# The setup of a fused decoder layer moves its loads into the places of the attention values, and batch 0 may load its values after the first half of them is made

## The chip, the cores and the metric

The kernel runs on one core of one Trainium2 chip. The metric is the device time of one execution in microseconds (us), lower is better. Unless said otherwise, times within a run are counted from the start of the profiled span.

The engines are called as the profile calls them: PE is TensorE (matrix products and transposes; PEld is its weight load), DVE is VectorE, ACT is ScalarE, POOL is GpSimd, and SP is the queue from which this kernel issues all its DMAs, in order.

## What is computed

The reference is a decoder layer in float32 on x of 16 batches x 512 tokens x 256 channels:

```
x = layernorm(x + self_attention(x))
x = layernorm(x + cross_attention(x, ctx))     # ctx: 16 batches x 64 rows x 256
x = layernorm(x + mixture_of_experts(x))       # 8 experts, 1024 hidden units each
```

The self attention is linear: per head, the products of keys and values over the tokens, for two sets of weights, are multiplied elementwise, and the queries are multiplied by that state. The cross attention, which the change touches, has 16 heads of 64 channels:

```
q = x @ Wq.T;  k, v = split(ctx @ Wkv.T)
attn = softmax(q k^T / 8 + mask)               # over the 64 context rows, per head
out = (attn v, heads side by side) @ Wout.T + b_out
```

In the expert layer each of the 8 experts takes the first 1024 tokens with a positive routing weight, in the order of the tokens.

## The kernel before, in words

**The work.** The batches go through the layer one by one, in stages that overlap. A setup makes what all batches need from the context. `context_keys` makes the keys and writes them to a DRAM scratch (`k_dram`). `output_weights` transposes Wout. `context_values` makes the values already multiplied by Wout, head by head, which the kernel calls v Wout, and writes them to `vo_dram`, in two halves: `context_values(0)` for batches 0 to 7 and `context_values(1)` for batches 8 to 15. So the cross attention of a batch ends in one large product of its probabilities with v Wout (L845, `ps_x`), and no output projection follows.

**A half of the values.** It has eight rounds (r = 0 to 7, two heads each). A round makes the values of 128 channels for 512 context rows (`context_rows`, L445, `ps_kv`), copies them to a tile `st`, and one round later `times_wout` multiplies them by Wout: for four groups g of two batches and two heads h it does one product each (L496, `ps_vo`). The eight results are copied by `evac` from PSUM to tiles `vst`, by ACT and DVE in turn (L186, L188), and SP writes them to `vo_dram` (L505). A `vst` holds two groups g, so a round uses two of these tiles and has four writes, of 64 partitions each.

**The places.** Tiles come from pools, and a tag in a pool has a fixed number of places; a new tile takes the place that is free first, and whoever writes it first waits for the last reader of the old tile. The tag "vo" of the pool `wk2` has six places of 4224 bytes per partition. `vst` uses them in the setup, and so do the batches' values `vo` later: `load_vo` (L789) reads a quarter of the heads and half of the context rows of one batch as one tile, in four DMAs of 32 partitions. A batch has eight such tiles: six are loaded ahead, the other two after the first two are used. The setup's other loads, the context `cn` (L424), the weights `nat` (L434) and `nato` (L528), use the tag "cn" of the pool `setup`, which has two places. That pool is closed when the routing of batch 0 begins, and the experts' pool takes its memory.

**The order of the work.** The program is written by a planner. Each stage is a generator (a stream); the class `Model` estimates what each traced instruction takes on its engine, and `weave` always continues the stream that is due first by its plan and is not waiting for something. The order that results is fixed for PE, DVE, ACT and POOL (`in_order`). The DMAs on SP are ordered by the framework's scheduler. A DMA on SP also waits for the DMA eight issues before it, since eight completion semaphores are used in turn. The eight PSUM banks (`bank`) are shared by all stages.

**What the change's steps touch.** `cross_attention` (L773 and following) first starts `load_vo` six times for every batch but batch 0; then it makes the scores (L819, `ps_sim`), the softmax in four steps per batch (L825 to L827, L805 to L809, ending in `pT`), and the product L845. Batch 0 waits after its softmax until `("values", 1)` is set, that is, until the second half has been traced, and loads its values only then. `all_routing` closes the setup's pool after batch 0's cross attention. `ranks` at the end counts the tokens of each expert with two products by constant matrices, `ones` and `before` (L898, L900), which POOL makes at the start of the program. The experts' first weights, `wi` and `wo_`, are loaded at L979 and L984 and first used at L941 (`ps_h`).

Of the kernel before, what the change touches and what calls it, by code (L numbers as in the profile page):

```python
# [9 lines left out]
FP = mybir.dt.float32  # L10
# [3 lines left out]
ALU = mybir.AluOpType  # L14
# [4 lines left out]
P = 128  # L19
# [97 lines left out]
def decoder_layer(  # L117
# [25 lines left out]
    nc = tc.nc  # L143

    B, S, C = x.shape
    J = context.shape[1]
    NT = S // P
    NC = C // P
# [11 lines left out]
    GB = 2  # L160
# [21 lines left out]
    def evac(dst, src):  # L182

        flip[0] ^= 1
        if flip[0]:
            nc.scalar.copy(dst, src)  # L186
        else:
            nc.vector.tensor_copy(dst, src)  # L188
# [7 lines left out]
    def col(name, src):  # L196
# [11 lines left out]
    eps = const.tile([P, 1], FP, tag="eps", name="eps")  # L208
    nc.gpsimd.memset(eps, EPS)

    ones = const.tile([P, P], FP, tag="ones", name="ones")
    nc.gpsimd.memset(ones, 1.0)

    before = const.tile([P, P], FP, tag="before", name="before")
    nc.gpsimd.affine_select(
        out=before, in_=ones, pattern=[[1, P]], compare_op=ALU.is_gt, fill=0.0,
        base=0, channel_multiplier=-1,
    )


    not_last = const.tile([P, 1], FP, tag="not_last", name="not_last")
    nc.vector.tensor_scalar(not_last, ident[:, P - 1:P], -1.0, 1.0, ALU.mult, ALU.add)
# [58 lines left out]
    with ExitStack() as att:  # L281
# [138 lines left out]
        BJ = B * J  # L420

        def load_context(sp, q):
            t = sp.tile([P, 4, C], FP, tag="cn", name="cn")
            nc.sync.dma_start(  # L424
                out=t,
                in_=context.rearrange("b j c -> (b j) c")[q * 512:(q + 1) * 512, :].rearrange(
                    "(i p) c -> p i c", p=P
                ),
            )
            return t  # L430

        def load_wkv(sp, r4):
            t = sp.tile([P, 4, C], FP, tag="cn", name="nat")
            nc.sync.dma_start(out=t, in_=x_wkv[r4 * 512:(r4 + 1) * 512, :].rearrange("(r p) c -> p r c", p=P))  # L434
            return t

# [49 lines left out]
        def context_values(q):  # L486


            def times_wout(r, st):
                for g in range(NG):  # L490
                    if g % 2 == 0:
                        vst = wk2.tile([P, 2, 2, CX], FP, tag="vo", name="vst", bufs=6)
                    for h in range(2):
                        hd = slice(h * J, (h + 1) * J)
                        ps = bank(f"ps_vo{h}")
                        nc.tensor.matmul(  # L496
                            ps[:, :CX], st[hd, g * P:(g + 1) * P], held["xwoutT"][hd, r, :], start=True, stop=True
                        )
                        evac(vst[:, g % 2, h, :], ps[:, :CX])
                    if g % 2 == 0:  # L500
                        continue
                    g0 = q * NG + g - 1
                    out_ = vo_dram[g0 * GB:(g0 + 2) * GB].rearrange("(g b) j h c -> b j g h c", b=GB)
                    for bl in range(GB):
                        nc.sync.dma_start(  # L505
                            out=out_[bl, :, :, r * 2:(r + 1) * 2, :].rearrange("j g h c -> j g (h c)"),
                            in_=vst[bl * J:(bl + 1) * J].rearrange("p g h c -> p g (h c)"),
                        )

            last = None  # L510
            for r in range(NP):
                st = context_rows(NP + r, q)
                yield
                if last is not None:
                    times_wout(*last)
                    yield
                last = r, st
            yield WAIT
            times_wout(*last)
            yield  # L520
            held["values", q] = True

        def output_weights():

            xwoutT = held["xwoutT"] = sp.tile([P, NP, CX], FP, tag="xwoutT", name="xwoutT", bufs=1)
            for hf in range(2):
                nato = sp.tile([P, NC, INNER // 2], FP, tag="cn", name="nato")
                nc.sync.dma_start(  # L528
                    out=nato,
                    in_=x_wout[:, hf * 512:(hf + 1) * 512].rearrange("(r p) c -> p r c", p=P),  # L530
                )
                for i2 in range(2):
                    ps = bank("ps_wo")
                    for i in range(2):
                        for oc in range(NC):
                            nc.tensor.transpose(
                                ps[:, i * C + oc * P:i * C + (oc + 1) * P],
                                nato[:, oc, (i2 * 2 + i) * P:(i2 * 2 + i + 1) * P], ident,
                            )
                    r = hf * 4 + i2 * 2  # L540
                    evac(xwoutT[:, r:r + 2, :C], ps.rearrange("p (i c) -> p i c", i=2))
                ps = bank("ps_wo")
                for i in range(NP // 2):
                    for oc in range(NC):
                        nc.tensor.matmul(
                            ps[:, i * E:(i + 1) * E], nato[:, oc, i * P:(i + 1) * P], m[:, oc, C:],
                            start=(oc == 0), stop=(oc == NC - 1),
                        )
                r = hf * NP // 2
                nc.vector.tensor_copy(  # L550
                    xwoutT[:, r:r + NP // 2, C:], ps[:, :NP // 2 * E].rearrange("p (r e) -> p r e", e=E)
                )
                yield
# [219 lines left out]
        def cross_attention(b, x1, x1T):  # L773
# [17 lines left out]
                    )  # L791
                vos.append(t)

            if b:
                for _ in range(6):
                    load_vo()

# [29 lines left out]
                beside(cross_st, softmax(t, s))  # L829
            yield from until(lambda: len(ready) == NT)  # L830
            yield from until(lambda: made(probsT))
            if b == 0:

                while ("values", 1) not in held:
                    yield 2.0
                for _ in range(6):
                    load_vo()
            yield from until(lambda: made(*vos))
            ps = [bank("ps_x") for _ in range(NT)]
            for c in range(8):  # L840
                for i in range(NH // 4):
# [44 lines left out]
        def ranks():  # L886

            place = wk1.tile([P, 6, NTT, E], FP, tag="kq", name="ranks")  # L890
            pos, tot, cum, nxt, start, rank = (place[:, i] for i in range(6))


            nc.vector.tensor_single_scalar(pos, w_all, FLT_MIN, ALU.is_ge)
            posf = pos.rearrange("p t e -> p (t e)")
            yield
            ps_tot = bank("ps_tot")
            nc.tensor.matmul(ps_tot, ones, posf, start=True, stop=True)  # L898
            ps_in = bank("ps_in")
            nc.tensor.matmul(ps_in, before, posf, start=True, stop=True)  # L900
            nc.vector.tensor_copy(tot.rearrange("p t e -> p (t e)"), ps_tot)
            nc.vector.tensor_copy(rank.rearrange("p t e -> p (t e)"), ps_in)
            yield
            src, s = tot, 1
            while s < NTT:
                nc.vector.tensor_copy(nxt[:, :s, :], src[:, :s, :])
                nc.vector.tensor_add(nxt[:, s:, :], src[:, s:, :], src[:, :NTT - s, :])
                src, nxt, s = nxt, (cum if src is tot else src), s * 2
                yield
            nc.vector.tensor_sub(start, src, tot)  # L910
            nc.vector.tensor_add(rank, rank, start)
            nc.vector.scalar_tensor_tensor(w_sel, rank, float(CAP), w_all, ALU.is_lt, ALU.mult)
            NB = B - HEAD_B
            least = small.tile([P, NB], FP, tag="least", name="least")
            nc.vector.tensor_reduce(
                least, start.rearrange("p (b t) e -> p b t e", t=NT)[:, HEAD_B:, 0, :], AX.X, ALU.min
            )
            nc.vector.tensor_single_scalar(least, least, float(CAP), ALU.is_lt)
            n_f = small.tile([P, 1], FP, tag="n_f", name="n_f")
            nc.vector.tensor_reduce(n_f, least, AX.X, ALU.add)  # L920
            nc.vector.tensor_copy(n_i, n_f)
            yield
# [122 lines left out]
        def made(*tiles):  # L1045
            return all(model.made[t.name][0] <= model.free["PE"] for t in tiles)

        def until(ready):
            while not ready():
                yield 0.5  # L1050
# [34 lines left out]
        def all_routing():  # L1085
            nonlocal ffn
            for b in range(B):
                routing_st.plan(SETUP + (b + 1) * STEP, STEP, 1.0)
                yield from until(lambda: finished["cross"] > b)
                if b == 0:  # L1090
                    setup.close()
                    ffn = pool(att, "ffn", 1)
                yield WAIT
                yield from routing(b, done.pop(b)[0])
                finished["routing"] = b + 1
            yield from ranks()
# [110 lines left out]
```

## Time and profile before

| | |
|---|---|
| median of 3 runs | 1412.0 us (1411.22 to 1413.67) |
| profiled execution, own time | 1410.71 us |
| its span | 1409.0 us |
| mean granted clock of PE over the span | 0.989 |
| PE busy | 1368.0 us |
| product with the values (L845), all batches | 241.0 us busy, 17.3 us idle before it |
| writes of v Wout (L505) | 64 DMAs of 264 KB, 3.9 us to landing (median) |
| loads of values (L789) | 512 DMAs of 132 KB, 4.2 us to landing (median) |

The profiled execution is one run of its own; its time is a little above its span, since work lies around the span. A row of a timeline gives the start, the duration, the engine, the line, the operation, the tiles (output<-input, buffer numbers left out), the shapes and the number of instructions; what stands in brackets is the idle time before it and what ended it. "PEclk" is the share of full clock that PE was granted. A float32 product is carried out in two passes, so the timeline counts two rows of L496 for each product of the program. Some records of products are missing from the trace.

### The profile page before, as it was taken

Reading aid. Unit: us, or ns where it says so; the run is one execution under the profiler, and the core shown is the slowest. Engines: PE = TensorE matmul, PEld = TensorE weight load, DVE = VectorE, ACT = ScalarE, POOL = GpSimd, SP = SyncE. Lnnn points to the kernel's source line nnn. Section 1 sums busy time; section 2 is a strip of 40 time slices with the busy share of each in tenths; the row PEclk is TensorE's granted clock in tenths of the full one; section 3 lists DMA queues with packets and bytes.
Section 4 is the critical chain, followed back from the end, with each engine's and each line's share of the span. In section 5 each row is a group of like instructions: output and inputs, shape, how many; then the busy total and the mean of one; then the engine's idle time right before and its main releaser. Section 6 shows DMA issues by size and latency. Waiting matters only on the chain.

```text
span 1409.0 us, 23950 instructions
## 1 busy us (share of the span) xinstructions
PE 1368.0 (97%) x9630; PEld 1083.8 (77%) x9630; DVE 848.5 (60%) x1953; ACT 400.2 (28%) x904; POOL 203.9 (14%) x140
## 2 busy tenths in 40 slices
PE   7999979999999999999999999999999999999996
PEld 5766656886978787887878787878888787878685
DVE  2445836558393747466483848475766848484842
ACT  1135232132232313232233323141423323232221
POOL 0001111102010111102020112112120202021200
PEclk9999989999999999999999999999999999999998
DMA  8657377420615144331706053413343061505220
GB/s 244 212 147 220 94 197 202 103 67 1 169 61 139 61 114 130 96 104 27 202 16 169 31 139 105 125 61 85 100 110 105 21 179 46 154 15 147 67 69 24
DMA packets 97284, 153.56 MB, mean 109 GB/s; under 512 B 14473, under 2 KB 69009, under 8 KB 97169
## 3 DMA queue, kind: packets, MB, share of 16 engines
q1 hardware_dynamic: 97168, 151.98, 38.8%
q8 instruction: 78, 1.28, 0.4%
q14 instruction: 38, 0.30, 0.1%
HBM read 114.71 MB, written 37.22 MB: 108 GB/s over the span
## 4 chain that ended last, share of the span: by engine, by line
PE 90%; DVE 4%; DMA 3%; ACT 1%; issue 1%; SPq 0%; DVEq 0%; ACTq 0%
PE ps_x L845 16%; PE ps_e L958 15%; PE ps_sim L819 15%; PE ps_h L941 14%; PE ps_p L719 4%; PE ps_gk L637 4%; PE ps_kv L445 4%; PE ps_o L695 3%; PE ps_t L242 2%; PE ps_kq L759 2%; PE ps_vo L496 2%; PE ps_s L649 2%; PE ps_g L563 2%; DMA vo<-vo_dram 1%; PE ps_zt L708 1%; PE ps_m L678 1%
## 5 line engine op out<-in xcount | busy, mean ns | idle before, releaser
L845 PE MATMUL ps_x<-vo,pT 32*128 32x264 f32 x4096 | 241.0, 389 | 17.3 <-DMA vo<-vo_dram 9.0
L845 PEld LDWEIGHTS ps_x<-vo,pT 32*128 32x128 f32 x4096 | 218.9, 189 | 38.1 <-issue 17.8
L941 PE MATMUL ps_h<-head_T,wi 128*128 128x256 f32 x1024 | 239.3, 379 | 1.8 <-DMA wi<-L_ffn_experts_inter_dram 1.8
L819 PE MATMUL ps_sim<-kq,x1T 128*128 128x512 f32 x512 | 235.0, 593 | 0.0
L941 PEld LDWEIGHTS ps_h<-head_T,wi 128*128 128x128 f32 x1024 | 193.4, 190 | 41.6 <-issue 13.6
L807 POOL TENSOR_TENSOR s<-s,sm 128x1024 f32<-128x1024 f32 x64 | 121.8, 1903 | 540.7 <-DVE sm L806 475.7
L852 DVE TENSOR_TENSOR x<-ps_x,x 128x264 f32<-128x264 f32 x64 | 23.2, 424 | 241.9 <-PE ps_x L845 241.9
L827 ACT ACTIVATE s<-s 128x512 f32<-128x512 f32 x128 | 80.6, 630 | 274.7 <-DVE s L826 274.7
L819 PEld LDWEIGHTS ps_sim<-kq,x1T 128*128 128x128 f32 x512 | 94.5, 190 | 82.4 <-issue 73.7
L825 DVE TENSOR_REDUCE mx<-ps_sim 128x8 f32<-128x512 f32 x128 | 86.1, 673 | 39.9 <-PE ps_sim L819 39.5
L826 DVE TENSOR_TENSOR s<-ps_sim,mx 128x512 f32<-128x512 f32 x128 | 88.5, 691 | 4.4
L733 POOL TENSOR_TENSOR x<-x,bout 128x1056 f32<-128x1056 f32 x16 | 38.8, 2423 | 359.2 <-ACT hT L947 172.6
L947 ACT ACTIVATE hT<-ps_h 128x256 f32<-128x256 f32 x128 | 46.7, 377 | 133.1 <-PE ps_h L941 133.0
L809 DVE STREAM_TRANSPOSE pT<-s 128x1024 f32<-128x1024 f32 x64 | 78.5, 1227 | 8.0 <-POOL s L807 8.0
L709 ACT ACTIVATE zT<-ps_zt,shift,gain 128x512 f32<-128x512 f32 x32 | 23.2, 776 | 192.1 <-PE ps_zt L708 192.1
L805 DVE TENSOR_REDUCE sm<-s 128x16 f32<-128x1024 f32 x64 | 77.0, 1204 | 0.0
L276 ACT ACTIVATE x<-x,off,rstd 128x264 f32<-128x264 f32 (+1 forms) x112 | 58.3, 591 | 29.9 <-DVE off L274 29.9
L695 PE MATMUL ps_o<-m,xT 128*128 128x264 f32 x256 | 66.7, 387 | 0.0
L949 DVE TENSOR_SCALAR hT<-ps_h 128x256 f32<-128x256 f32 x128 | 51.7, 408 | 23.7 <-PE ps_h L941 23.6
L270 ACT ACTIVATE rstd<-bn_mv,eps 128x4 f32<-128x4 f32 (+1 forms) x66 | 19.5, 295 | 153.4 <-DVE bn_mv L259 150.6
L719 PE MATMUL ps_p<-wo,zT 128*128 128x264 f32 x256 | 62.8, 386 | 0.0
L445 PE MATMUL ps_kv<-cT,wT 128*128 128x512 f32 x128 | 61.5, 614 | 0.0
(172 smaller groups left out, 1887.7 us busy)
## 6 DMA issues: line engine op xcount, KB each, us to landing
vo<-vo_dram SPq DMA_DIRECT2D x512, 132.0 KB, 4.2
vo_dram<-vst SPq DMA_DIRECT2D x64, 264.0 KB, 3.9
xt<-in_x_dram SPq DMA_DIRECT2D x16, 512.0 KB, 4.0
wi<-L_ffn_experts_inter_dram SPq DMA_DIRECT2D x8, 1024.0 KB, 5.0
gx<-in_x_dram SPq DMA_DIRECT2D x15, 512.0 KB, 5.5
x_rest<-x SPq DMA_DIRECT2D x14, 512.0 KB, 3.0
out_dram<-x SPq DMA_DIRECT2D x14, 512.0 KB, 2.9
k_dram<-st SPq DMA_DIRECT2D x16, 256.0 KB, 2.5
```

The lines of the kernel that those rows point to most:

```text
L445: nc.tensor.matmul(ps, wT[:, cc, r % 4 * P:(r % 4 + 1) * P], cT[:, cc, q * 512:(q + 1) * 512], start=(cc == 0), stop=(cc == NC - 1),)
L695: nc.tensor.matmul(ps[:, :CX], xT[:, cc, t * P:(t + 1) * P], m[:, cc, :], start=(cc == 0), stop=(cc == NC - 1))
L719: nc.tensor.matmul(ps[:, :CX], zT[:, cc, t * P:(t + 1) * P], wo[:, cc, :], start=(cc == 0), stop=(cc == NC - 1))
L807: nc.gpsimd.tensor_mul(s, s, sm.unsqueeze(2).to_broadcast([P, NH, J]))
L809: nc.vector.transpose(probsT[:, :, t, :], s.rearrange("p h (a j) -> p (h a) j", a=2))
L819: nc.tensor.matmul(ps, x1T[:, cc, t * P:(t + 1) * P], kq[:, cc, hf * 512:(hf + 1) * 512], start=(cc == 0), stop=(cc == NC - 1),)
L825: nc.vector.tensor_reduce(mx[:, hs], sim, AX.X, ALU.max)
L826: nc.vector.tensor_sub(s[:, hs, :], sim, mx[:, hs].unsqueeze(2).to_broadcast([P, 8, J]))
L827: nc.scalar.activation(s[:, hs, :], s[:, hs, :], AF.Exp, scale=SCALE)
L845: nc.tensor.matmul(ps[q][:, :CX], probsT[pq, blk].rearrange("p t i -> p (t i)"), vos[c][pq, i, :], start=(c == 0 and i == 0), stop=(c == 7 ...
L941: nc.tensor.matmul(ps[:, :TB], wi[:, cc, f * P:(f + 1) * P], head_T[b][:, cc, t0 * P:t0 * P + TB], start=(cc == 0), stop=(cc == NC - 1),)
L958: nc.tensor.matmul(ps[:, :C], hT[f][:, t * P:(t + 1) * P], wo_[:, f, :], start=(f == 0), stop=(f == NF - 1),)
```

## The change

It does five things. The setup's loads `cn`, `nat` and `nato` take places of the tag "vo" in `wk2` (six) in place of "cn" in the setup's pool (two). `vst` gets a tag and four places of its own in the setup's pool, each for one group g, so a round has eight writes of 64 partitions in place of four, each with half the bytes. The six early `load_vo` of every batch become a stream of their own that starts when the batch's own half of the values is traced; batch 0 no longer waits for the second half. The closing of the setup's pool now waits for the second half as well as for batch 0's cross attention. And `ones` and `before` are no longer kept from the start: `ranks` makes them at the end, in a seventh part of its tile, with the same two POOL instructions.

```diff
-    ones = const.tile([P, P], FP, tag="ones", name="ones")
-    nc.gpsimd.memset(ones, 1.0)
-    before = const.tile([P, P], FP, tag="before", name="before")
-    nc.gpsimd.affine_select(out=before, in_=ones, ...)
...
         def load_context(sp, q):
-            t = sp.tile([P, 4, C], FP, tag="cn", name="cn")
+            t = wk2.tile([P, 4, C], FP, tag="vo", name="cn", bufs=6)
...
         def load_wkv(sp, r4):
-            t = sp.tile([P, 4, C], FP, tag="cn", name="nat")
+            t = wk2.tile([P, 4, C], FP, tag="vo", name="nat", bufs=6)
...
             def times_wout(r, st):
                 for g in range(NG):
-                    if g % 2 == 0:
-                        vst = wk2.tile([P, 2, 2, CX], FP, tag="vo", name="vst", bufs=6)
+                    vst = sp.tile([P, 2, CX], FP, tag="vst", name="vst", bufs=4)
                     for h in range(2):
...
-                        evac(vst[:, g % 2, h, :], ps[:, :CX])
-                    if g % 2 == 0:
-                        continue
-                    g0 = q * NG + g - 1
-                    out_ = vo_dram[g0 * GB:(g0 + 2) * GB].rearrange("(g b) j h c -> b j g h c", b=GB)
+                        evac(vst[:, h, :], ps[:, :CX])
                     for bl in range(GB):
                         nc.sync.dma_start(
-                            out=out_[bl, :, :, r * 2:(r + 1) * 2, :].rearrange("j g h c -> j g (h c)"),
-                            in_=vst[bl * J:(bl + 1) * J].rearrange("p g h c -> p g (h c)"),
+                            out=vo_dram[(q * NG + g) * GB + bl, :, r * 2:(r + 1) * 2, :],
+                            in_=vst[bl * J:(bl + 1) * J],
                         )
...
-                nato = sp.tile([P, NC, INNER // 2], FP, tag="cn", name="nato")
+                nato = wk2.tile([P, NC, INNER // 2], FP, tag="vo", name="nato", bufs=6)
...
-            if b:
+            def load_first():
+                yield from until(lambda: ("values", b // (B // 2)) in held)
                 for _ in range(6):
                     load_vo()
+
+            beside(cross_st, load_first())
...
-            if b == 0:
-                while ("values", 1) not in held:
-                    yield 2.0
-                for _ in range(6):
-                    load_vo()
-            yield from until(lambda: made(*vos))
+            yield from until(lambda: len(vos) == 6 and made(*vos))
...
-            place = wk1.tile([P, 6, NTT, E], FP, tag="kq", name="ranks")
+            place = wk1.tile([P, 7, NTT, E], FP, tag="kq", name="ranks")
+            consts = place[:, 6].rearrange("p t e -> p (t e)")
+            ones, before = consts[:, :P], consts[:, P:2 * P]
+            nc.gpsimd.memset(ones, 1.0)
+            nc.gpsimd.affine_select(out=before, in_=ones, ...)
...
-                yield from until(lambda: finished["cross"] > b)
+                yield from until(lambda: finished["cross"] > b and ("values", 1) in held)
```

## The prediction

> **What bounds the kernel now.** I read the page first: it gives the bound and how full the other engines are.
>
> ```profile
> PE 1368.0 (97%) x9630; PEld 1083.8 (77%) x9630; DVE 848.5 (60%) x1953; ACT 400.2 (28%) x904; POOL 203.9 (14%) x140
> ```
>
> TensorE is busy 1368.0 of 1409.0 us, so an edit pays only where it shortens the 41 us in which PE stands still, or the stretches in which PE runs slowly. The waits of PE (us in total, times, longest) say where those are:
>
> ```profile
> PE ps_x L845 <- DMA vo<-vo_dram: 9.0, 2, 8.3
> PE ps_x L845 <- DVE pT L809: 3.2, 1, 3.2
> PE ps_x L845 <- DVE rm L874: 3.1, 1, 3.1
> PE ps_h L941 <- DMA wi<-L_ffn_experts_inter_dram: 1.8, 1, 1.8
> PE ps_t L242 <- DMA nat<-in_L_xattn_Wkv_dram: 0.9, 1, 0.9
> ```
>
> The largest is the wait for the values. The PE timeline (start, duration) puts it in batch 0; the last row is batch 3, a stage with no wait:
>
> ```profile
> 192.51 0.71 PE L845 MATMUL ps_x<-vo,pT 32*128 32x264 f32 x2
> 201.54 16.22 PE L845 MATMUL ps_x<-vo,pT 32*128 32x264 f32 x226 [8.33 <-DMA vo<-vo_dram]
> 218.44 2.70 PE L845 MATMUL ps_x<-vo,pT 32*128 32x264 f32 x28 [0.68 <-DMA vo<-vo_dram]
> 237.03 1.10 PE L941 MATMUL ps_h<-head_T,wi 128*128 128x256 f32 x4 [1.77 <-DMA wi<-L_ffn_experts_inter_dram]
> ...
> 425.95 14.52 PE L845 MATMUL ps_x<-vo,pT 32*128 32x264 f32 x256
> ```
>
> Batch 0's product with the values runs from 192.51 to 221.14 (218.44 + 2.70), 28.6 us for work that takes 14.5 in batch 3: 14.1 us lost, of which 9.0 are wait. The rest is the clock, as the table of stretches shows (PEclk is the third number from the end):
>
> ```profile
> 196.00:201.00 5.00, 0.00 (x0) 0.00 (x0) 0.00 (x0) 0.00 (x0) 0.00 (x0) 0.56 1.02 284
> 203.00:205.00 2.00, 2.00 (x24) 1.77 (x20) 0.00 (x0) 0.00 (x0) 0.00 (x0) 0.50 1.01 243
> 208.00:210.00 2.00, 2.00 (x43) 1.93 (x40) 0.00 (x0) 0.00 (x0) 0.00 (x0) 1.00 0.94 262
> ```
>
> PE runs at half clock until about 206.5. The DMA engines are full meanwhile (share 1.02, 284 GB/s): one burst of loads that could have been spread. Why they came late is on SP's queue:
>
> ```profile
> 191.51 3.06 SPq L505 DMA_DIRECT2D vo_dram<-vst  x4
> 194.66 0.76 SPq L308 DMA_DIRECT2D gx<-in_x_dram  x1
> 195.47 18.40 SPq L789 DMA_DIRECT2D vo<-vo_dram  x31
> ```
>
> All loads of batch 0 but one are issued after the last write of the second half, for the places "vo" are shared with `vst`. Last, the copies that feed those writes:
>
> ```profile
> L505 SPq DMA_DIRECT2D vo_dram<-vst x64: 574/640/1517, 81.9 to 193.5; - x64
> DMA to landing us min/median/max: 3.0/3.9/5.4
> ```
>
> **What the Trainium skill says.** "TensorE: Matmul & The Clock Gate", Part 1: The HAM clock gate: an idle window of about 3.4 us halves the clock, and a busy window of about that length restores it. The trace agrees: after 8.33 us idle the clock was 0.50 for some 5 us, and after 3.12 us idle (batch 1) the same stage took 16.3 us in place of 14.5. "DMA: Bandwidth & Descriptors", Anatomy of one DMA: the fixed cost of a transfer (about 2 us, fitted for another issue path) is mostly the receipt of the write. The trace agrees in kind: no `vst` write landed in under 3.0 us. So halving a write doesn't halve its landing. That page, How many engines, lets 64 partitions use all 16 engines; the 64-partition writes here moved 248 GB/s.
>
> **The change part by part.** The built programs' instruction orders give what moves; durations are from before.
>
> *The values' wait.* In the new order, batch 0's 24 first loads stand right behind round 1 (of 0 to 7) of the second half's writes, and its product behind round 6. From the start of the last round of the first half (111.2) PE has up to the end of round 1: 3 rounds x 2.0, 3 ps_kv pairs x 1.8, ps_p 3.7, two transpose groups 1.9, ps_gt and ps_g 1.9, in all 18.9, so 130; with the copies and eight issues the loads start near 134. 24 x 132 KB = 3.2 MB at 284 GB/s take 11.5 us, so they are down by about 147. Up to the product come another 5 rounds (10.0), 5 ps_kv (9.0), all of ps_sim (13.8), ps_kq 3.8, ps_gk 3.7, ps_o 3.7, and 5.0 + 1.1 of small groups, in all 50: it comes near 180. The cover is 33 us, so the loads cost nothing. If that cover fell away, the 14.1 us would come back. Saved: 14.1.
>
> *The experts' first weights.* `wi` (issued 230.74, 6.2 us to land) stood behind 24 loads of batch 1, which started only as batch 0's places came free. In the new order these run beside batch 0's product and 21 us of PE work follows before L941. The 1.77 us go; some of it may reappear in batch 1's wait for VectorE, which is next. I take 1.5 (0 to 1.8).
>
> *The setup's loads.* With six places instead of two, the four `nat` loads need not wait for a transpose. The first is issued near 8.1 instead of 10.31 and is ahead of `wv`; by its 5.5 us it is there at 13.6, before PE asks at 14.9. Saved 0.9 (0 to 0.9). `wv`, `wo` and the small vectors go some 10 us later on SP and are first needed at 54: nothing.
>
> *Writes by single g.* 64 issues become 128, half the bytes each, the same packets. What one costs lies between 0.30 us (the shortest `vo` load, same bytes) and 0.64 (the old write): 2.4 to 5.1 us a round on SP, which has 4.8 a round. I take 0.35. Work on SP alone is hidden as long as it fits in that.
>
> *The ring of four.* This is the added wait: a copy into `vst` (ACT and DVE in turn) waits until the writes of the same g one round earlier have landed; queued behind it are the copies of the key/value product, the softmax on DVE and the normalizations on ACT, and PE waits for those and for PSUM banks. One place turns in copy 0.43 + issue + landing: at least 0.43+0.30+3.0 = 3.7 us, at most 0.43+2x0.6+5.4 = 7.0; I take 0.43+0.35+3.4 = 4.2. The rounds' PE starts in the first half (79.8, 85.1, 89.9, 94.7, 99.5, 104.3, 108.2, 111.2) with a 0.9 us transpose group moved ahead of the last give gaps 5.3, 4.8, 4.8, 4.8, 4.8, 3.9, 4.0: 0.5 us short in all at 4.2, and 17 us at 7.0. In the second half only two gaps are as short (4.8 each): 0 at 4.2, 4.4 at 7.0. I take 1.0 us (0 to 21).
>
> *Batch 0's product moved ahead.* From the last similarity matmul of batch 0 to the product, the new PE order holds 2.8 (ps_o) + 1.8 + 2.0 + 1.0 + 1.8 + 2.0 + 1.8 + 1.0 + 2.0 = 16.2 us. Before, the fourth pT was ready 12.9 us after that matmul (171.0 to 183.9), and VectorE was full:
>
> ```profile
> 150.00:160.00 10.00, 10.00 (x41) 5.65 (x40) 9.15 (x17) 2.96 (x6) 1.90 (x1) 1.00 0.14 49
> 170.00:180.00 10.00, 9.64 (x39) 5.31 (x39) 9.76 (x20) 3.21 (x9) 0.46 (x1) 1.00 0.19 59
> ```
>
> (the third pair is DVE). Now round 5's copies stand ahead of that transpose. They need round 4's writes down, which SP issues behind a `gx` load that waits for PE: about 13.4, so pT at 14.6, in time; but round 6's copies, which free the banks for the product, come at 17 to 18. So 1 to 2 us of wait; bounds 0 and 7.7 (6 of wait and 1.7 of half clock). I take 2.0.
>
> *The rest.* The matmuls, copies and bytes are the same, and from batch 2 on the orders agree. `ones` and `before` are made at the end, on a POOL that has been idle since 1335 when PE wants them at 1364.8: nothing; without that cover it would be 0.5 us, from the 0.21 and 0.30 rows of before. Batch 1's own wait (3.1 and 1.8 of slow clock) keeps its DVE chain: I take no change (-4.9 to +3).
>
> Sum: 14.1 + 1.5 + 0.9 - 1.0 - 2.0 = 13.5. The profiled execution took 1410.7 us (span 1409.0), so 1397.2; the median of the runs is 1.3 above the profiled one: 1398.5.
>
> **The rivals.**
> - *The wait moves to VectorE.* The product stands one stage earlier and so nearer to a 92% full DVE. If pT or the banks are 6 us late, half clock follows: 7.7 instead of 2.0, gain 7.8, 1404.2. For it: the DVE shares above, and copies that now block on DMAs. Against: the 3.3 us between 12.9 and 16.2.
> - *The ring of four decides, and it is slower.* Place: the `vst` copies at L496's rounds. If a place turns in 7.0 us (the 5.4 us landing always, and both issues in series), 21 us come against 16.5 saved: +4.9, with the run offset 1416.9. It decides from about 6.6 us a turn. For it: DMA share 0.8 in these rounds already. Against: the median landing of twice the bytes was 3.9.
> - *Batch 1's wait goes as well*, since its softmax now starts later after the product than before: up to 4.9 more, 1394 or below.
> - *The loads don't come early*, since SP is in order and something ahead of them waits: then 1411 to 1412. Against: in the new order only writes that are complete and an `xt` whose place is free by then stand ahead.
>
> **How the numbers follow.** Forecast 1398.5 with 1394.5 to 1402: 0.56. VectorE rival, 1402 to 1409: 0.24. More than that gained: 0.08. Loads not early: 0.05. Slower by the ring: 0.07. The range 1394 to 1406 holds the forecast, most of the first rival and a little of the third, 0.79. A measurement can tell about 0.2% (2.8 us) from no change: faster 0.88, same 0.05, slower 0.07.
>
> **What would show it.** No PE wait for `vo` and PEclk 1.00 through batch 0's product, which takes 14.5 to 15 us near 180; `vo` loads on SP near 134; no wait for `wi` or the first `nat`. The ring shows as waits of ACT and DVE copies into `vst` on the `vo_dram<-vst` writes; a few tenths each is right, and a landing above 4.5 us with PE waits at L496 makes me wrong. The VectorE rival would show as PE waiting at L845 for pT or for a copy.

## The result, and the profile after

The changed kernel takes 1398.1 us (median of 6 runs, 1396.2 to 1401.7) against 1412.8 us beside it (1409.3 to 1415.7): a ratio of 0.990 with a 95% interval of 0.9883 to 0.9916, 14.7 us less. The forecast was 1398.5. The profiled execution took 1397.24 us (span 1395.6), 13.5 less than the profiled execution before. The number is right, but the sum behind it is not: two errors cancelled, as the trace shows and the experiments below confirm.

The page's first part, busy time by engine:

```profile
PE 1365.0 (98%) x9630; PEld 1077.3 (77%) x9630; DVE 849.4 (61%) x1953; ACT 399.8 (29%) x904; POOL 203.7 (15%) x140
```

The waits of PE (us in total, times, longest), from the largest; there is no row left for `vo` or `wi`, but there is one for `nat`, and new small ones at L486, which was L496 before:

```profile
PE ps_x L828 <- DVE pT L798: 3.7, 2, 3.2
PE ps_rw L379 <- DVE early L376: 3.2, 1, 3.2
...
PE ps_t L233 <- DMA nat<-in_L_xattn_Wkv_dram: 1.0, 1, 1.0
PE ps_vo L486 <- DVE u L564: 0.8, 1, 0.8
PE ps_vo L486 <- ACT st L186: 0.7, 1, 0.7
...
PE ps_vo L486 <- ACT vst L186: 0.5, 1, 0.5
```

PE's timeline (start, duration, in brackets the idle time before) of what the prediction named: the first `nat` transposes, batch 0's product, the first use of `wi`, and batch 1's product (L828 was L845, L932 was L941):

```profile
14.95 1.97 PE L233 MATMUL ps_t<-ident,nat 128*128 128x128 f32 x8 [1.01 <-DMA nat<-in_L_xattn_Wkv_dram]
...
189.44 15.16 PE L828 MATMUL ps_x<-vo,pT 32*128 32x264 f32 x256
...
228.72 1.03 PE L932 MATMUL ps_h<-head_T,wi 128*128 128x256 f32 x4
...
253.29 14.52 PE L828 MATMUL ps_x<-vo,pT 32*128 32x264 f32 x256 [0.49 <-DVE pT L798]
```

Batch 0's product takes 15.2 us without a wait, where it took 28.6; `wi` is there in time. But batch 1's wait of 3.1 us has fallen to 0.5, and its product takes 14.5 in place of 16.3. The prediction's sum held that wait unchanged; only one of its rivals had it go.

SP's queue (start, time from the first issue to the end of the last, number) shows the loads early, and something else:

```profile
84.81 33.36 SPq L491 DMA_DIRECT2D vo_dram<-vst  x50
118.28 0.52 SPq L299 DMA_DIRECT2D gx<-in_x_dram  x1
118.91 4.97 SPq L491 DMA_DIRECT2D vo_dram<-vst  x8
123.94 0.57 SPq L775 DMA_DIRECT2D vo<-vo_dram  x1
128.24 11.61 SPq L491 DMA_DIRECT2D vo_dram<-vst  x16
139.96 0.52 SPq L605 DMA_DIRECT2D xt<-in_x_dram  x1
140.53 13.13 SPq L775 DMA_DIRECT2D vo<-vo_dram  x23
```

From 84.8 on SP issues 50 writes in 33.4 us almost without a pause, 0.67 us each, so the 8 writes of a round take 5.3 us. PE has 4.8 us of work in a round. In this stretch SP waits 2.4 us in all for copies and never for an earlier DMA, so the eight semaphores used in turn are not what holds it. The tile `vst` says the same from the other side: what ended the idle time of the engines that copy into it, and the landing of its writes.

```profile
L491 SPq DMA_DIRECT2D vo_dram<-vst x128: 445/548/1997, 81.0 to 217.3; - x128
...
  DMA vo_dram<-vst: 42.8, 46
...
DMA to landing us min/median/max: 2.2/2.4/4.2
```

A write lands in 2.4 us, sooner than the 3.4 that I took. Yet ACT and DVE stood 42.8 us before `vst`, since the writes of the place that they wanted had been issued late. At the first of these waits the copy stood from 86.95 to 87.86 for a write that was issued at 85.39 and landed at 87.76. In the first half the second write of a tile was issued 2.2 us (median) after the tile's copies were done; in `one_write`, an experiment below, its one write follows them after 0.15 us. When a wait began the write was always out already: the late issue shows as a wait for its landing.

**The balance of the two profiled executions.** From the start of the first round of v Wout (79.80 before, 79.17 after) to the first use of `wi` (237.03, 228.72) the stage went from 157.23 to 149.55 us: 7.7 gained, where my terms for it (14.1, 1.5, -1.0, -2.0) made 12.6. From there to batch 1's product 27.27 became 24.57, and the product itself 1.8 less: 4.5. Batch 2's product took 14.52 in place of 16.21 after the same wait of 3.2: 1.7. The start gave 0.6. From the start of the last block of expert products (`ps_e`) to the end it took 17.2 in place of 16.1: -1.1. Together 13.4, the difference of the spans.

### The profile page after: what moved, and what is told of

The parts are those of the page before. It is cut to its first block, busy times and chain, and to the rows that moved or that the text cites. A ratio compares the mean times of both kernels' runs of the same rounds, so it can differ in the third digit from the quotient of the medians.

```text
span 1395.6 us, 24180 instructions
## 1 busy us (share of the span) xinstructions
PE 1365.0 (98%) x9630; PEld 1077.3 (77%) x9630; DVE 849.4 (61%) x1953; ACT 399.8 (29%) x904; POOL 203.7 (15%) x140
## 2 busy tenths in 40 slices
DMA packets 98309, 153.57 MB, mean 110 GB/s; under 512 B 15497, under 2 KB 70033, under 8 KB 98193
## 4 chain that ended last, share of the span: by engine, by line
PE 90%; DVE 5%; DMA 2%; ACT 1%; SPq 1%; issue 1%; DVEq 0%; ACTq 0%
PE ps_x L828 16%; PE ps_e L949 15%; PE ps_sim L808 15%; PE ps_h L932 14%; PE ps_gk L623 4%; PE ps_p L705 4%; PE ps_o L681 3%; PE ps_kv L436 3%; PE ps_t L233 2%; PE ps_kq L745 2%; PE ps_vo L486 2%; PE ps_s L635 2%; PE ps_g L549 2%; PE ps_zt L694 1%; PE ps_m L664 1%; PE ps_g L554 1%
## 5 line engine op out<-in xcount | busy, mean ns | idle before, releaser
L932 PE MATMUL ps_h<-head_T,wi 128*128 128x256 f32 x1024 | 238.9, 379 | 0.0
L828 PE MATMUL ps_x<-vo,pT 32*128 32x264 f32 x4096 | 233.1, 383 | 5.7 <-DVE pT L798 3.7
L828 PEld LDWEIGHTS ps_x<-vo,pT 32*128 32x128 f32 x4096 | 212.1, 185 | 25.6 <-issue 5.6
L932 PEld LDWEIGHTS ps_h<-head_T,wi 128*128 128x128 f32 x1024 | 193.4, 190 | 38.8 <-issue 12.7
L940 DVE TENSOR_SCALAR hT<-ps_h 128x256 f32<-128x256 f32 x128 | 51.7, 408 | 22.2 <-PE ps_h L932 22.1
```

The lines of the kernel that those rows point to most:

```text
L828: nc.tensor.matmul(ps[q][:, :CX], probsT[pq, blk].rearrange("p t i -> p (t i)"), vos[c][pq, i, :], start=(c == 0 and i == 0), stop=(c == 7 ...
L932: nc.tensor.matmul(ps[:, :TB], wi[:, cc, f * P:(f + 1) * P], head_T[b][:, cc, t0 * P:t0 * P + TB], start=(cc == 0), stop=(cc == NC - 1),)
```

## The experiments

Three things are open: whether the early loads carry the gain; what the ring of four and its writes cost, and by which mechanism; and where batch 1's wait went. The theory after the trace was: the early loads carry it, the issues on SP cost some 6 us, and batch 1's wait had been VectorE standing beside GpSimd. Where two kernels have the same order of instructions on an engine, the text says so.

### Batch 0's loads late again

Two kernels. `late_trace` only delays the tracing of batch 0's values; `late_all` also puts the writes of the last two rounds into the values' places, so that the loads can't come before them.

```diff
             def load_first():
-                yield from until(lambda: ("values", b // (B // 2)) in held)
+                yield from until(lambda: ("values", b // (B // 2) if b else 1) in held)
```

and in `late_all` also

```diff
-                    vst = sp.tile([P, 2, CX], FP, tag="vst", name="vst", bufs=4)
+                    if q and r >= NP - 2:
+                        vst = wk2.tile([P, 2, CX], FP, tag="vo", name="vst", bufs=6)
+                    else:
+                        vst = sp.tile([P, 2, CX], FP, tag="vst", name="vst", bufs=4)
```

> The changed kernel with one thing undone: batch 0's values are traced only after the second half, and the tiles of the last two rounds of that half take the places of the values, so that none of batch 0's 24 loads can be issued before those writes. Theory 1 (the early loads of batch 0 carry the gain): the product of batch 0 loses its 13.4 us again, the wait for wi (1.8) comes back, and with it batch 1's wait (some 4 us), while the ring of four costs a little less since its last two rounds are free of it: 1411 to 1418 us, no longer faster than the kernel before. Rival (the setup's loads and the places of its own for v Wout carry it): 1398 to 1402.

> The changed kernel, with batch 0's values traced only after the second half, but all places as in the change. In the instruction order of this kernel 19 of batch 0's 24 loads still stand ahead of the second half's later writes. Theory 1 (what brings the loads forward is that their places are free, the condition in the stream does not matter): the product of batch 0 waits under 3 us for values, 1397 to 1403 us. Rival (the condition does it): the 9 us wait for the values comes back, 1408 to 1416.

Measured: `late_all` 1421.8 us (1419.4 to 1425.3), ratio to before 1.0068, interval 1.0043 to 1.0094: slower than before, and above what I expected. Two parts of that expectation failed as well: neither the wait for `wi` nor batch 1's wait came back (batch 1 waits 0.50 us in its trace). `late_trace` 1413.2 us (1408.5 to 1415.3, the profiled one the fastest of them), ratio 1.0002, interval 0.9988 to 1.0016. So the change without its early loads, in the order of instructions that comes with them being late, is slower than the kernel before. The two kernels have the same order on PE, DVE, ACT and POOL; they differ in when the values arrive and in where `vst` of two rounds lies, which did not shorten its waits (47.3 us in `late_all`, 43.3 in `late_trace`). The PE row of batch 0's product in `late_all`:

```profile
213.84 20.11 PE L831 MATMUL ps_x<-vo,pT 32*128 32x264 f32 x256 [7.98 <-DMA vo<-vo_dram]
```

and PE rows of `late_trace`, with that product and the largest waits of PE between the first round and `wi`:

```profile
158.07 0.83 PE L486 MATMUL ps_vo<-xwoutT,st 64*128 64x264 f32 x2 [3.00 <-DVE xT L188]
...
193.80 1.09 PE L694 MATMUL ps_zt<-ident,z 128*128 128x128 f32 x8 [1.89 <-ACT vst L186]
...
203.31 15.05 PE L828 MATMUL ps_x<-vo,pT 32*128 32x264 f32 x256
...
220.26 0.33 PE L233 MATMUL ps_t<-ident,x 128*128 128x128 f32 x1 [1.65 <-ACT x L267]
```

Early loads save 7.98 of wait and 5.06 of slow clock (20.11 - 15.05), 13.0 us in the traces and 8.6 between the medians. For `late_trace` both theories failed in part. The mechanism was that of the first (19 of the 24 loads come early, because their places are free, and the product waits for none), the time was that of the rival. Its product comes 13.9 us later than in the changed kernel (203.3 against 189.4), behind all eight rounds, and from the first round to `wi` PE stands still 8.8 us in place of 3.0. The condition in the stream therefore matters through the order that the planner makes of it. That 14.5 us of PE work without copies, put between two rounds of v Wout, is what helps, is my reading and not shown: the largest of the waits stands 45 us ahead of the product.

### The writes: fewer, more, and one place more

Three kernels with the changed kernel's order on all engines but SP; there the scheduler also moves batch 0's loads (the first is issued at 86.5 us in `one_write`, 123.9 in the changed kernel, 162.2 in `four_writes`). `one_write` has one write of 128 partitions for each group g:

```diff
-                    for bl in range(GB):
-                        nc.sync.dma_start(
-                            out=vo_dram[(q * NG + g) * GB + bl, :, r * 2:(r + 1) * 2, :],
-                            in_=vst[bl * J:(bl + 1) * J],
-                        )
+                    b0 = (q * NG + g) * GB
+                    nc.sync.dma_start(
+                        out=vo_dram[b0:b0 + GB, :, r * 2:(r + 1) * 2, :].rearrange("b j h c -> (b j) (h c)"),
+                        in_=vst.rearrange("p h c -> p (h c)"),
+                    )
```

> The changed kernel with one write of 128 partitions for each group g in place of two of 64: 64 issues instead of 128 over both halves, the same bytes and places; the orders on TensorE, VectorE, ScalarE and GpSimd are the same. Theory 1 (in the rounds of v Wout the issues on SP are the bound, 8 x 0.64 = 5.1 us a round against 4.8 of TensorE's work): the copies' waits for vst fall from 42.8 us to under 15 and most of the 5.5 us that the rounds cost come back: 1392.5 to 1395.5. Rival (the landing or the DMA engines' throughput is the bound; twice the bytes land later, so places turn no faster): the waits stay at 35 to 50 us, 1397 to 1401.

`four_writes` cuts each of the two writes in two of 32 partitions:

```diff
                     for bl in range(GB):
-                        nc.sync.dma_start(
-                            out=vo_dram[(q * NG + g) * GB + bl, :, r * 2:(r + 1) * 2, :],
-                            in_=vst[bl * J:(bl + 1) * J],
-                        )
+                        for j0 in range(0, J, J // 2):
+                            nc.sync.dma_start(
+                                out=vo_dram[(q * NG + g) * GB + bl, j0:j0 + J // 2, r * 2:(r + 1) * 2, :],
+                                in_=vst[bl * J + j0:bl * J + j0 + J // 2],
+                            )
```

> The changed kernel with four writes of 32 partitions for each group g in place of two of 64: 256 issues instead of 128 over both halves, the same bytes, places and orders on TensorE, VectorE, ScalarE and GpSimd. Theory 1 (the number of issues on SP sets the pace of the ring): 16 issues of 0.35 to 0.5 us are 5.6 to 8 us a round against 4.8 of TensorE's work, so nearly every round is late by 1 to 3 us: waits for vst above 70 us, 1404 to 1416 us. Rival (the landing, or the bytes, set it; a quarter of the partitions lands no later): 1396 to 1401.

`ring_five` has five places (a small tile `last` gives its spare copies for the memory):

```diff
-                    vst = sp.tile([P, 2, CX], FP, tag="vst", name="vst", bufs=4)
+                    vst = sp.tile([P, 2, CX], FP, tag="vst", name="vst", bufs=5)
```

> The changed kernel with five places for the tiles of v Wout in place of four; the order of instructions is the same on every engine. Theory 1 (the issues on SP set the rate): a fifth place takes up one group's delay, 1.3 us, at the start of each half, and does nothing to the rate: waits for vst 30 to 42 us, 1396 to 1398. Rival (the number of places is the bound): a place may turn in 5/4 of the time, and the waits fall below 15 us: 1392.5 to 1395.

| issues a round | kernel | median, us | ratio to before, 95% | waits for `vst`, us | landing, us |
|---|---|---|---|---|---|
| 4 | `one_write` | 1392.2 | 0.986 (0.9841 to 0.9879) | 6.9 | 2.7 |
| 8 | changed kernel | 1398.1 | 0.990 (0.9883 to 0.9916) | 42.8 | 2.4 |
| 16 | `four_writes` | 1433.3 | 1.0144 (1.0109 to 1.0179) | 78.2 | 1.7 |
| 8, five places | `ring_five` | 1399.6 | 0.991 (0.9892 to 0.9928) | 22.1 | 2.4 |

The first three move the same bytes through the same places. Their times follow the number of issues, while the landing goes the other way: the smallest writes land soonest and make the slowest kernel. The rows of `vst` in `one_write`:

```profile
L491 SPq DMA_DIRECT2D vo_dram<-vst x64: 319/370/1320, 79.6 to 204.1; - x64
...
  DMA vo_dram<-vst: 6.9, 17
...
DMA to landing us min/median/max: 2.0/2.7/5.0
```

and in `four_writes`:

```profile
L492 SPq DMA_DIRECT2D vo_dram<-vst x256: 302/422/1657, 82.1 to 245.9; - x128
...
  DMA vo_dram<-vst: 78.2, 55
...
DMA to landing us min/median/max: 1.6/1.7/4.1
```

The DMA engines are not what is full: in the stretch from 85 to 100 us of `four_writes` their share (second number from the end) is 0.55, at 139 GB/s, while PE has gaps (13.35 busy of 15).

```profile
85.00:100.00 15.00, 13.35 (x62) 7.39 (x60) 5.60 (x14) 4.11 (x10) 0.00 (x0) 1.00 0.55 139
```

The same stretch of `one_write`, where PE (the third number) is busy all the 15 us:

```profile
85.00:100.00 15.00, 15.00 (x76) 9.18 (x75) 9.54 (x25) 5.69 (x15) 0.00 (x0) 1.00 0.80 280
```

This decides for the issues on SP, against the landing and against full DMA engines. `one_write` is faster than both given kernels, 0.3 us below the lower end of what was expected (1392.5). `four_writes` lies 17 us above the upper end of my expectation: SP needs 0.48 us a write (36 in 17.29 us), 7.7 us a round, at the upper end of what I had assumed, and I had left out the clock. The stretch from the first round to `wi`, in `four_writes` and then in the changed kernel, shows it:

```profile
80.28:258.13 177.85, 162.18 (x924) 106.42 (x924) 93.69 (x216) 56.37 (x135) 19.53 (x14) 0.93 0.64 168
...
79.17:228.72 149.55, 146.55 (x924) 98.42 (x924) 92.14 (x211) 55.40 (x134) 17.93 (x14) 1.00 0.80 202
```

PE stands still 15.7 us in place of 3.0, and its mean clock is 0.93 in place of 1.00, which by my estimate (0.07 of 177.85) is some 12 us more of the 28.3. Batch 0's product takes 20.0 us there, and a wait of 1.9 us for `wi` is back. So the cost does not grow evenly with the issues: once PE has gaps, the slower clock comes on top.

`ring_five` met neither theory. The waits fell by half, and the stage from the first round to `wi` is 147.1 us in its trace, 2.5 less than in the changed kernel, so a place more does absorb part of the lateness. But the time is not distinguishable from that of four places; in its profiled execution the start was 2.6 us later (81.72 against 79.17), and the products of batch 2 (16.2 against 14.5) and of the last batch (16.3 against 14.6) each took 1.7 us longer, none of which the fifth place touches.

With one write and five places, nothing should be left to gain:

> The changed kernel with one write of 128 partitions for each group and five places instead of four; orders as in the changed kernel on all engines but SP. Theory 1 (the issues on SP were the bound; with four issues a round nothing of weight is left of the ring): waits for vst fall from 6.9 us to under 3, and the time stays at that of one write with four places, 1391 to 1393.5. Rival (the number of places still binds): 1387 to 1390.

Measured: 1392.2 us (1391.0 to 1397.2), ratio 0.9856, interval 0.983 to 0.9882; waits for `vst` 1.2 us. As expected of theory 1: the last 5.7 us of such waits had cost nothing that can be measured.

### One write in the order of `late_trace`

The edit is that of `one_write`, in `late_trace`.

> The kernel in which batch 0's values are traced after the second half (its loads still come early), with one write of 128 partitions per group; orders as there on all engines but SP. That kernel took 1413.2 us though its product waits for no values. Theory 1 (in its order the rounds of the second half stand close together, and the ring of four with its SP issues eats what the early loads save): more comes back than the 5.9 us of the changed kernel's order, 1402 to 1406. Rival (waits of that order which the writes have nothing to do with, the transposes behind ScalarE's normalization and the xT copy): 1407 to 1412.

Measured: 1405.9 us (1402.5 to 1411.2), ratio 0.9945, interval 0.9925 to 0.9965, that is 7.4 less than `late_trace`. It is within theory 1, at its upper end, and the 7.4 are not distinguishable from the 5.9 of the changed kernel's order. What the writes did not cause stays: its trace still has the wait of 3.0 for `xT` and 2.0 for the normalized x, and batch 0's product takes 17.2 us, 1.5 of them a wait for values. The 13.7 us between the medians of this kernel and `one_write` (12.0 by their ratios to before) come with the condition, the only edit between them, and so with the order.

### The setup's loads alone, in the kernel before

```diff
-            t = sp.tile([P, 4, C], FP, tag="cn", name="nat")
+            t = wk2.tile([P, 4, C], FP, tag="vo", name="nat", bufs=6)
```

and the same for `cn` and `nato`.

> The kernel before with one part of the change: the setup's loads cn, nat and nato take the six places of the values. Orders are the same on all engines but SP. Theory 1 (the loads come earlier but share full DMA engines, so they only move the wait): the start of the first round of v Wout within 1.5 us of before, 1411 to 1414 us. Rival (these loads carry a part of the gain, as the prediction's 0.9 us and more): 1408 to 1411.

Measured: 1412.3 us, ratio 0.9998, interval 0.998 to 1.0016: no difference that can be measured. In its profiled execution the `nat` wait is gone, but the wait for `early` just before it (L388) is 4.8 in place of 3.6. That need not be a consequence: in `before_pool_sub`, which leaves these loads alone, it is 4.8 too. The start of the first round, 78.3 here and 79.8 before, is no measure of it either: in eight kernels whose PE order is the same up to that point (the changed kernel, `one_write`, `one_write_five`, `ring_five`, `four_writes`, `late_all`, `late_trace`, `late_trace_one_write`) it lies between 77.8 and 82.7 without a pattern.

### Batch 1's wait

In the kernel before, the last steps on VectorE (and on POOL) ahead of batch 1's product at 264.30 were:

```profile
259.64 0.19 DVE L870 TENSOR_REDUCE rm<-w_all 128x4 f32<-128x32 f32 x1
259.72 2.34 POOL L713 TENSOR_TENSOR xt<-xt,bo 128x1024 f32<-128x1024 f32 x1
259.86 2.25 DVE L871 TENSOR_TENSOR w_all<-w_all,rm 128x32 f32<-128x32 f32 x1
...
262.92 1.23 DVE L809 STREAM_TRANSPOSE pT<-s 128x1024 f32<-128x1024 f32 x1
```

L871 takes 2.25 us here for 32 elements, and ends with GpSimd's addition. In the changed kernel the same instruction comes 0.37 us ahead of that addition and takes 0.19; the transpose that lies beside the addition is not slowed:

```profile
250.97 0.19 DVE L854 TENSOR_TENSOR w_all<-w_all,rm 128x32 f32<-128x32 f32 x1
251.34 2.35 POOL L699 TENSOR_TENSOR xt<-xt,bo 128x1024 f32<-128x1024 f32 x1
...
252.00 1.23 DVE L798 STREAM_TRANSPOSE pT<-s 128x1024 f32<-128x1024 f32 x1
```

The Trainium skill, "SBUF — State Buffer", SBUF: two separate sides, says this: a VectorE operation with two SBUF inputs and a GpSimd operation that reads SBUF share a pair of ports under an exclusive lock, and the one that starts second stands until the first is done. The traces agree: L871 has two SBUF inputs, the transpose one. To test whether that made the wait, the kernel before was built with this one instruction on GpSimd, ahead of the addition; everything else keeps its order.

```diff
-            nc.vector.tensor_sub(w, w, mbc)
+            (nc.gpsimd if b == 0 else nc.vector).tensor_sub(w, w, mbc)
```

> The kernel before with one instruction moved: for batch 0's routing the subtraction of the row maximum (w_all, L871) runs on GpSimd, ahead of its large addition L713, and no longer on VectorE beside it; the order of everything else is kept. Theory 1 (batch 1's wait for pT, 3.1 us and 1.8 of slow clock, came from VectorE standing 2.1 us at that instruction while GpSimd added): batch 1's wait falls to about 1 us, its product takes 14.5 us, 1408 to 1410. Rival (the wait came with the late weights wi, which left VectorE idle for 1.5 us): the wait stays at 3 us, 1411.5 to 1414.

```profile
259.44 0.24 POOL L871 TENSOR_TENSOR w_all<-w_all,rm 128x32 f32<-128x32 f32 x1 [0.35 <-DVE rm L870]
...
259.83 2.35 POOL L713 TENSOR_TENSOR xt<-xt,bo 128x1024 f32<-128x1024 f32 x1
260.27 1.24 DVE L809 STREAM_TRANSPOSE pT<-s 128x1024 f32<-128x1024 f32 x1
...
261.66 14.63 PE L845 MATMUL ps_x<-vo,pT 32*128 32x264 f32 x256 [0.95 <-DVE pT L809]
```

Measured: 1408.8 us (1403.9 to 1412.8), ratio 0.9964, interval 0.9951 to 0.9978. The wait is 0.95 and the product 14.63, as theory 1 said, though the wait for `wi` (2.2 here) is still there; the rival falls. `setup_loads` says the same: its wait for `wi` was 3.5 us, twice that of before, and batch 1's wait was 3.12 all the same, with 2.25 us at L871. So about 4 us of the change's gain (3.9 between the medians, 5.1 by the ratio) were an accident of timing that one moved instruction would have brought without the change. The slower clock after the wait is not a fixed part of it: in `setup_loads` the product behind the same 3.12 us took 14.63, not 16.32.

## Why the prediction was right, and where its sum was wrong

- **The values' wait, 14.1.** Right. The trace gives 13.4 (28.6 to 15.2), and the loads were out long before the product: all issued by 153.7, the product at 189.4. They start at 123.9 and 140.5, not near 134, and the product comes at 189, not near 180, because SP and the rounds were slower than assumed. The two `late` kernels put the effect at 8.6 (medians) to 13.0 (traces). It needs the new order too: `late_trace`, where the product waits for no values either, is no faster than before.
- **`wi`, 1.5.** Right: the full 1.77 is gone.
- **The first `nat` wait, 0.9.** Wrong in kind, of no size. The load was issued at 8.5 in place of 10.3, near the predicted 8.1, but I kept its landing at 5.5 us. With four such loads at once it was 6.4 to 8.5, so PE still waited 1.01. `setup_loads` shows that this part of the change is worth nothing measurable.
- **SP's issues, 0.35 each, "hidden".** This is the step that failed. I took it near the shortest `vo` load; the write took 0.55 at the median and 0.67 with the gap. My own bounds (2.4 to 5.1 us a round, against 4.8) had 5.1 at their end, and the measured 5.3 is just past it: from there SP is the bound and each bound round is late by the difference. "The same packets" was not right either: 64 more writes brought 1024 more packets of under 512 B (14473 to 15497).
- **The ring of four, -1.0.** Wrong size and wrong mechanism. The term had a copy, an issue and a landing of 3.4; the landing was 2.4, and the place was late because the issue was. The ring and the issues together cost 6.7 us in the traces (149.55 against 142.88 in `one_write`, first round to `wi`) and 5.9 between the medians, in place of 1.0. Of the 6.7, 0.6 stand in batch 0's product (15.16 against 14.52). PE's own waits at L486 are only 2.2 us; the rest shows as weights loaded late (4.4 us before L486) and as rounds that last longer while PE counts as busy (3.2 to 3.3 us at 114.3 and 186.3, 2.05 at 124.8).
- **Batch 0's product moved ahead, -2.0.** Right in size, by luck; the place was wrong. I had the product wait for banks behind round 6's copies, and it waits for nothing, here and in `one_write`. In `one_write`, where the ring no longer costs, the stage takes 142.88; before, without its 14.1 and 1.77, it would be 141.36. That leaves -1.5, and two waits of such a size stand ahead of the product, at L486 (0.71 at 170.2, 0.84 at 176.4). This is a difference of two traces, not a test.
- **Batch 1's own wait, 0.** Wrong: +4.5 in the trace, 3.9 to 5.1 by `before_pool_sub`. I had kept its chain on VectorE as it was and overlooked that a 0.2 us instruction in it took 2.25. It was the rival "batch 1's wait goes as well", but for another cause than that rival named.
- **`ones` and `before`, 0.** Right: from batch 3's product to the product with `ones` (L889, L898 before) it is 938.9 us as before.

So 5.7 too little cost for the ring (6.7 - 1.0) stood against 4.5 too little gain at batch 1; the remaining differences are within what two executions differ by. Batch 2's 1.7 us is of that kind: its product took 16.21 after the same 3.2 us wait in `one_write`, `ring_five`, `late_trace` and `late_trace_one_write`, and 14.52 in `one_write_five` and `before_pool_sub` (17.4 in `four_writes`, 17.6 in `setup_loads`). The rival in which VectorE becomes the bound didn't come: PE had no wait for `pT` or the banks at batch 0. The rival in which the ring decides named the right place, and `four_writes` shows that it can end on the other side; its price came from the landing, while the true one is the issue.

What stays open: why a write of 64 partitions holds SP longer (0.55) than one of 128 partitions with the same rows (0.37); and which part of the new order is worth the 12 to 14 us. That the writes could be shared with another engine's queue was not run, since the order of the program changes with it.

## What to carry to other kernels

Count a DMA queue's issues as work in a stage, at the duration of the same shape, and compare it with the stage's period: at 5.3 against 4.8 us a finer write cost 6 us, and one DMA over 128 partitions in place of two over 64 gave it back. When an instruction of 0.2 us stands at 2 us in a row, look at GpSimd beside it before you take the chain's length as given. And when a forecast comes true, check its terms in the trace: here the gain of the early loads, the cost of the ring and an unrelated stall added up to the forecast by accident.

## What the runs showed of the hardware that was not expected

- SP's time for a write follows its shape and not its bytes alone: 0.42 us for 32 partitions x 528, 0.55 for 64, 0.37 for 128, 0.64 for 64 x 2 x 528 (medians). The skill's page "DMA: Bandwidth & Descriptors", Rules for kernel authors, says not to use two transfers to disjoint partition halves, since they share the same engines; the runs agree (1398.1 against 1392.2) and add the issue as a reason.
- In the changed kernel the DMA engines were busier (share 0.90 from 85 to 100 us) while they moved less (208 GB/s) than in `one_write` (0.80, 280 GB/s).
- The landing of a write fell with its size after all, from 3.9 us (264 KB from 64 partitions, before) to 2.4 (132 KB) and 1.7 (66 KB), where the prediction had a floor of 3.0; 264 KB from 128 partitions took 2.7. The load on the DMA engines differed between these kernels, so size is not the only difference.
- The same idle time of 3.25 us before batch 2's product was followed by a product of 14.52 us in three traces (the changed kernel, `one_write_five`, `before_pool_sub`) and of 16.0 to 17.6 in the other eight; why is open.
- Each further write brought 16 packets of under 512 B: 14473 of them before, 15497 with 64 more writes, 17544 with 192 more.
